# An edge-gated graph kernel: additions a tile ahead, edge sums two steps behind, z kept in the rows of h

## The chip, the cores and the metric

The kernel runs on one core of a Trainium2 chip. The metric is the time of one execution on the device in microseconds (us): the median of seven runs for the kernel before. One further execution was taken by the profiler, and all lines of the profile come from it.

Engines are named as in the profile: PE is TensorE (matmul), PEld its weight loads, DVE is VectorE, ACT is ScalarE, POOL is GpSimd and SP is SyncE, which here only issues DMA transfers. L12 is line 12 of the kernel.

## The reference

x is 16 batches of 1024 nodes with 256 features; adj is a sparse 1024 x 1024 matrix (about nine entries a column). Cut to what matters:

```python
pre_u = einsum('bud,dk->buk', x, W1[:256])
pre_v = einsum('bvd,dk->bvk', x, W1[256:])
hidden = relu(pre_u[:, :, None, :] + pre_v[:, None, :, :] + b1)
S = sigmoid(einsum('buvk,ko->buvo', hidden, W2)[..., 0] + b2)
a = einsum('buv,bud->bvd', S * adj, x)          # gated edge sums
m = einsum('uv,bud->bvd', adj, x) * x            # plain edge sums, times x
out = beta1 * x + beta2 * (a @ Wa + ba) + beta3 * (m @ Wm + bm)
```

S is needed only where adj has an entry, so the kernel works on lists of edges.

## The kernel before, in words

**Tiling.** The 16 batches form 4 groups of 4 (g), the 1024 target nodes 8 blocks of 128 (vt). A block (g, vt) is worked on as 10 tiles of up to 128 edges each: two windows of 64 targets (w), five tiles a window (j). There are 32 blocks and 320 tiles; tile n is tile s = n % 10 of block k = n // 10. Of the 32 blocks, 0 to 15 belong to groups 0 and 1, 16 to 23 to group 2 and 24 to 31 to group 3.

**A tile.** `fetch` (L496, an indirect DMA issued by POOL) gathers for each edge one row of 8 KB out of a table in DRAM: 1024 numbers of pre_u (four batches) and the 1024 numbers of x. The rows land in one of NF = 6 buffers `fetched`. `expand` (L569, two matmuls) spreads pre_v + b1 of the targets (`X`) over the edges into PSUM (`pc`, two buffers). `gate` adds both into `t` (L601), and four operations `t = max(t, 0) * W2` with an accumulated sum give a score for each edge and batch (L606). ScalarE takes the sigmoid (L609) and scales the columns of `left`, which already hold the edge's adj value (`left_adj`, L579), by it (L612). `aggregate` (L623) multiplies `left` with the x half of the fetched rows and sums over edges in PSUM (`acc`).

**A block.** `half_end` (L631) copies a finished `acc` to SBUF (`ev`), `turn_over` transposes it on TensorE (L641), copies the result into `LT` (L644) and later multiplies the plain sums by x (`times_h`, L654). `block_end` multiplies `LT` with Wa and Wm (L672) into a PSUM tile `pz`, ScalarE copies that to `z` (L675), VectorE adds beta1 * h (L676) from the rows `h_blk` loaded by SP (L775), and SP stores z (L678).

**Work laid beside it.** `halves` makes X for the next block (products L427 and L431, copies L461, L462, L465, L468, subtraction L463). `rows` makes pre_u for a table that a later block fetches from (product L427, copy L443, store L446); its place is written out by hand in `plan`, as (load of x transposed, first half, second half), for blocks up to tile 233. `lists` makes the edge lists of a target block, in pieces that `fill` puts between the operations of `gate`.

**The order.** Every engine's instructions run in the order in which the loop over n writes them; there is no scheduler. `after(step, f)` puts f into a queue that `do(step)` runs. PSUM for products, transposes and pz is a pool of two banks (`misc`, made by `small`); a new tile takes a bank whose last tile has been read, as far as the order written so far says.

In step n the kernel before writes the edge sums of tile n - 1 (and the fetch for tile n + 5, which takes the buffer just read), the gate of tile n, then `do(n)`, the expansion for tile n + 2, and after these the transposes, products and their copies:

```python
        if 1 <= n <= total:
            aggregate(n - 1)
            fetch_val(2)
            if n - 1 + NF < total:
                fetch(n - 1 + NF)
            ...
        if n < total:
            gate(n)
```

Of the kernel before, what the change touches and what calls it, by code (L numbers as in the profile page):

```python
# [17 lines left out]
def kernel(  # L18
# [207 lines left out]

    NF = 6
    EARLY = 4  # L230
    fetched = []
    for i in range(NF):
# [146 lines left out]
    def fetch_val(n):  # L379

        for i, j in wanted[:n]:
            nc.gpsimd.indirect_dma_start(  # L382
                out=val[:, i, j:j + 1], out_offset=None, in_=adj_flat,
                in_offset=bass.IndirectOffsetOnAxis(ap=vidx[:, i, j:j + 1], axis=0),
                bounds_check=N * N - 1, oob_is_err=False)
        del wanted[:n]
# [12 lines left out]
    def after(step, f):  # L399
        due.setdefault(step, []).append(f)  # L400
# [191 lines left out]
    def fill(n, gap=True):  # L592
        for r in running:
            if r[1] == gap and r[2] <= n:
                piece_of(r, n)
                break

    def gate(n):
        k, g, vt, w, j = where(n)
        t = one.tile([P, GB, D], FP, name="t")  # L600
        nc.vector.tensor_tensor(t, fetched[n % NF][:, :GD].rearrange("p (b d) -> p b d", b=GB),  # L601
                                pcs.pop(n).rearrange("p (b d) -> p b d", b=GB), ALU.add)
        sc = wk.tile([P, GB], FP, name="sc")
        for b in range(GB):
            fill(n)
            nc.vector.scalar_tensor_tensor(t[:, b, :], t[:, b, :], 0.0, w2_b,  # L606
                                           ALU.max, ALU.mult, accum_out=sc[:, b:b + 1])
        gt = wk.tile([P, GB], FP, name="gt")
        nc.scalar.activation(gt, sc, AF.Sigmoid, bias=b2_b)  # L609
        for b in range(GB):  # L610
            m = len(QUARTERS[j])
            nc.scalar.activation(lefts[n][:, :m, b, 1, :], lefts[n][:, :m, b, 0, :], AF.Copy, scale=gt[:, b:b + 1])  # L612
# [15 lines left out]
    def half_end(n, q):  # L628

        evs[q] = one.tile([P, 2, D], FP, name=f"ev{q}")  # L630
        nc.scalar.copy(evs[q], accs.pop(q))  # L631

    def turn_over(k, w, q, step):
        if w == 0 and q == 0:
            LTs[k] = one.tile([P, DC, GB, 2, P], FP, name="LT")
        LT = LTs[k]
        pt = small("pt")
        ev = evs.pop(q)
        for i in range(4):
            r, c = divmod(i, DC)  # L640
            nc.tensor.transpose(pt[:, i * P:(i + 1) * P], ev[:, r, c * P:(c + 1) * P], ident)  # L641
        v = slice(w * W + q * U, w * W + (q + 1) * U)
        r = (w * W + q * U) // V
        nc.scalar.copy(LT.rearrange("p c b k (r v) -> p r (c b k) v", v=V)[:, r:r + 2],  # L644
                       pt.rearrange("p (r i v) -> p r i v", r=2, v=V))
        apart = k == BS - 1 and w == NW - 1
        if not apart:
            if not q:
                return
            v = slice(w * W, (w + 1) * W)  # L650

        def times_h():
            m = LT[:, :, :, 0, v]
            nc.vector.tensor_tensor(m, m, hTs[order[k]].rearrange("p b c n -> p c b n")[:, :, :, v], ALU.mult)  # L654
            if w == NW - 1 and q == 1:
                del hTs[order[k]]
        after(step + (1 if k == BS - 1 else 2), times_h)

    def block_end(k):

        g, vt = order[k]
        hb = hbs[k]
        z = big.tile([P, GB, D], FP, name="z", bufs=1)
        for h in range(2):
            for i, wt in ((1, w_a), (0, w_m)):
                step = yield
                if i:
                    pz = small("pz")
                    add_row(pz, bias_p)
                for bb in range(2):  # L670
                    for c in range(DC):
                        nc.tensor.matmul(pz[:, bb * D:(bb + 1) * D], LTs[k][:, c, 2 * h + bb, i, :], wt[:, c, :],  # L672
                                         start=False, stop=(i == 0 and c == DC - 1), skip_group_check=True)
            sl = slice(2 * h, 2 * h + 2)
            nc.scalar.copy(z[:, sl], pz.rearrange("p (b d) -> p b d", b=2))  # L675
            after(step + 2, lambda sl=sl: nc.vector.scalar_tensor_tensor(z[:, sl], hb[:, sl], be1, z[:, sl],  # L676
                                                                         ALU.mult, ALU.add))
        after(step + 3, lambda: nc.sync.dma_start(  # L678
            out[g * GB:(g + 1) * GB, vt * P:(vt + 1) * P, :].rearrange("b p d -> p b d"), z))
        del hbs[k], LTs[k]  # L680


# [43 lines left out]
    def plan(blocks, ns):  # L726

        for k, (load, *pieces) in zip(blocks, ns):
# [4 lines left out]
                     (43, 50, 52)))  # L733
    plan([(2, vt) for vt in range(NT)], ((60 + 10 * i, 68 + 10 * i, 71 + 10 * i) for i in range(NT)))
    plan([(3, vt) for vt in range(NT)], ((141, 149, 151), (149, 158, 161), *((153 + 10 * i, 161 + 10 * i, 168 + 10 * i)
                                                                             for i in range(2, NT - 1)), (223, 231, 233)))
    plan(again, ((103,), (113,), (125,), (133,)))
    begun = set(turn[:NT])
    end = parts = piece = last = None
# [2 lines left out]
        expand(n)  # L742
    left_adj(0)
    total = BS * T
    for n in range(total + 2):
        k, s = divmod(n, T)
        if 1 <= n <= total:
            aggregate(n - 1)
            fetch_val(2)
            if n - 1 + NF < total:  # L750
                fetch(n - 1 + NF)
            if n % TW in (0, MID + 1):
                half_end(n - 1, 0 if n % TW else 1)
        if n < total:
            gate(n)
            if n + 1 < total:
                left_adj(n + 1)
        if n % TW == 1 and n // TW + 1 < total // TW:
            load_mark(n // TW + 1)
        do(n)  # L760
        if n + 2 < total:
            expand(n + 2)
        if n == 1:
            w_a = load_weights(Wa, "w_a", nc.sync)
            w_m = load_weights(Wm, "w_m", nc.sync)
            bias = load_rows(bm, D, "bias", nc.sync)
            ba_b = load_rows(ba, D, "ba_b", nc.sync)
            be1 = load_rows(beta1, 1, "be1", nc.sync)
            be2 = load_rows(beta2, 1, "be2", nc.sync)
            be3 = load_rows(beta3, 1, "be3", nc.sync)  # L770
            after(10, scale_late)
        if s == 0 and 0 < k < BS:
            hbs[k - 1] = big.tile([P, GB, D], FP, name="h_blk", bufs=1)
            g, vt = order[k - 1]
            nc.sync.dma_start(hbs[k - 1], x_rows[vt * P:(vt + 1) * P, g * GB:(g + 1) * GB, :])  # L775
        if n == total - 6:
            hbs[BS - 1] = hts.tile([P, GB, DC, P], FP, name="hT").rearrange("p b c n -> p b (c n)")
            for v, m, f in tails:
                for h, o in tail_rows(x, v, m, f):
                    nc.sync.dma_start(h, o)  # L780
        for i in advance.get(n, ()):
            next(made[i], None)
        if n in start_list:
            running.append([made[start_list[n]], True, n])
            piece_of(running[-1], n)
        fill(n, False)
        if (s == 1 and 0 < k < BS) or n == total:
            turn_over(k - 1, 1, 1, n)
        if s in (3, 4, 5, 6) and 0 < k < BS:
            if s == 3:  # L790
                end = block_end(k - 1)
                next(end)
            go(end, n)
        if s == 7 and k < BS:
            turn_over(k, 0, 0, n)
            turn_over(k, 0, 1, n)
        if s == 9 and k < BS:
            turn_over(k, 1, 0, n)
        if n == total - 2:
            end = tail(tails[:2], n)  # L800
            next(end)
        elif n == total - 1:
            go(end, n)
        elif n >= total:
            end = tail([tails[2 + n - total]], n)
            next(end)
            go(end, n)
            go(end, n)
        if k + 1 < BS and s in (0, 2, 3, 5, 6):
            if s == 0:  # L810
                parts = halves(k + 1)
                next(parts)
            go(parts, n)
        if n in loads:
            if loads[n] in begun and loads[n][0] == 1:
                aside_.remove(loads[n])
            load_hT(loads[n])
            if loads[n] not in begun:
                copy_h(loads[n])
                begun.add(loads[n])  # L820
        if n in at:
            if at[n] != last:
                last = at[n]
                piece = rows(last)
                next(piece)
            go(piece, n)
        if n == 120:
            nc.gpsimd.partition_all_reduce(longest, rest, P, bass_isa.ReduceOp.max)
            after(n + 12, count_rest)
# [114 lines left out]
```

## Time and profile before

| What | Value |
|---|---|
| median of 7 runs | 1168.84 us (1165.89 to 1171.88) |
| profiled execution: time, span | 1167.33 us, 1165.4 us |
| busy share PE, DVE, ACT, POOL | 94%, 91%, 77%, 38% |
| mean granted TensorE clock | 0.976 |
| DMA: bytes, mean rate | 391.40 MB, 336 GB/s |

The span is the time from the first to the last instruction. The profile's page gives the busy time of each engine and the costliest groups of instructions, each with its count, its mean duration and the idle time before it with what ended that. The windows view gives busy times for stretches of the span. The timeline gives each instruction's start and duration, equal ones that follow each other merged ("x8"); in brackets stands idle time before it and what ended it. Matmuls are pipelined and their ends modelled, so TensorE's work is best read from starts. The waits view has lines "engine tile line <- what ended the wait: us in total, times, longest us".

### The profile page before, as it was taken

What the parts mean: (1) busy time and instruction counts of PE and PEld (TensorE: products, weight loads), DVE (VectorE), ACT (ScalarE), POOL (GpSimd) and SP (SyncE); (2) the same over time, 40 slices, a digit from 0 to 9 for tenths busy, and PEclk for the clock granted to TensorE, in tenths of its full rate; (3) what the DMA queues carried; (4) which work ended last, traced back from release to release, by engine and by line L of the source; (5) the groups of instructions that cost most, each with busy time, mean ns of one, the idle gap of its engine ahead of it and who ended that gap; (6) DMA issues with size and microseconds to landing.
All of it is one profiled execution on the core that took longest, in us unless ns stands there. A gap on an engine that the chain in (4) does not pass through costs nothing. (4 is left out here: it accounts for less than half of the span.)

```text
span 1165.4 us, 23918 instructions
## 1 busy us (share of the span) xinstructions
PE 1092.9 (94%) x7633; PEld 723.5 (62%) x7633; DVE 1056.3 (91%) x3487; ACT 894.2 (77%) x2624; POOL 439.6 (38%) x428
## 2 busy tenths in 40 slices
PE   7767899998999999999999999999999999999986
PEld 6644666665666666666666666666666666666553
DVE  7688889878999989989999999999999999999994
ACT  2346587777877877878888888888888888888873
POOL 1557645263335323443333333333333333333330
PEclk9968899999999999999999999999999999999999
DMA  9996899999999999999999999999999999999992
GB/s 283 304 311 221 276 379 335 346 307 344 355 313 331 381 380 337 361 345 384 386 370 367 363 366 356 359 372 380 361 373 339 357 325 334 333 340 328 326 338 69
DMA packets 147047, 391.40 MB, mean 336 GB/s; under 512 B 16752, under 2 KB 105328, under 8 KB 110704
## 3 DMA queue, kind: packets, MB, share of 16 engines
q0 software_dynamic: 50016, 300.50, 69.3%
q1 hardware_dynamic: 81616, 74.99, 20.1%
q10 hardware_dynamic: 15280, 14.29, 3.8%
q8 instruction: 63, 1.03, 0.4%
q14 instruction: 72, 0.59, 0.1%
HBM read 393.78 MB, written 50.33 MB: 381 GB/s over the span
## 5 line engine op out<-in xcount | busy, mean ns | idle before, releaser
L496 POOL DMA_INDIRECT fetched<-table,uidx x320 | 340.3, 1064 | 628.3 <-PE acc L623 463.5
L606 DVE SCALAR_TENSOR_TENSOR t<-t,w_b 128x256 f32<-128x256 f32 x1280 | 478.7, 422 | 19.3 <-ACT left L612 0.5
L601 DVE TENSOR_TENSOR t<-fetched,pc 128x1024 f32<-128x1024 f32 x320 | 389.5, 1217 | 42.9 <-PE pc L569 10.7
L623 PE MATMUL acc<-fetched,left 128*32 128x256 f32 x4096 | 335.6, 391 | 32.5 <-ACT left L612 26.8
L612 ACT ACTIVATE left<-left,gt 128x32 f32<-128x32 f32 (+1 forms) x1280 | 299.3, 304 | 10.4
L569 PE MATMUL pc<-X,mark 128*128 128x512 f32 x640 | 238.4, 455 | 6.2 <-ACT mark L562 5.0
L623 PEld LDWEIGHTS acc<-fetched,left 128*32 128x32 f32 x4096 | 129.8, 109 | 180.0 <-issue 55.4
L569 PEld LDWEIGHTS pc<-X,mark 128*128 128x128 f32 x640 | 97.3, 191 | 140.1 <-issue 88.1
L609 ACT ACTIVATE gt<-sc,b_b 128x4 f32<-128x4 f32 x320 | 96.2, 301 | 40.5 <-DVE t L606 35.9
L672 PE MATMUL misc<-w_m,LT 128*128 128x256 f32 x496 | 117.2, 379 | 0.0
L672 PE MATMUL misc<-w_a,LT 128*128 128x256 f32 x496 | 117.1, 379 | 0.0
L579 ACT ACTIVATE left<-onehot,val 128x128 f32<-128x128 bf16 (+1 forms) x320 | 116.5, 364 | 0.0
L427 PE MATMUL misc<-w_v,hT 128*128 128x256 f32 x448 | 107.4, 383 | 0.0
L427 PE MATMUL misc<-w_u,hT 128*128 128x256 f32 x416 | 101.4, 391 | 5.6 <-issue 3.6
L606 DVE DVE_READ_ACCUMULATOR t<-t,w_b 128x1 f32 x1280 | 104.3, 81 | 0.0
L672 PEld LDWEIGHTS misc<-w_a,LT 128*128 128x128 f32 x496 | 93.9, 189 | 15.1
L672 PEld LDWEIGHTS misc<-w_m,LT 128*128 128x128 f32 x496 | 93.8, 189 | 14.9
L382 POOL DMA_INDIRECT val<-in_adjT_dram,vidx x80 | 86.5, 1081 | 34.9 <-issue 22.0
L427 PEld LDWEIGHTS misc<-w_v,hT 128*128 128x128 f32 x448 | 86.0, 192 | 13.9
L427 PEld LDWEIGHTS misc<-w_u,hT 128*128 128x128 f32 x416 | 80.1, 196 | 17.2 <-issue 3.7
L631 ACT COPY ev<-acc 128x512 f32<-128x512 f32 x128 | 75.5, 590 | 14.1 <-PE acc L623 3.7
L641 PE MATMUL misc<-ident,ev 128*128 128x128 f32 x512 | 74.0, 276 | 5.6 <-ACT L L342 2.8
(164 smaller groups left out, 911.7 us busy)
## 6 DMA issues: line engine op xcount, KB each, us to landing
h_blk<-in_x_dram SPq DMA_DIRECT2D x31, 512.0 KB
out_dram<-z SPq DMA_DIRECT2D x31, 512.0 KB
hT<-in_xT_dram SPq DMA_DIRECT2D x28, 512.0 KB
table<-in_x_dram ACTq DMA_DIRECT2D x24, 512.0 KB
table<-tab SPq DMA_DIRECT2D x24, 512.0 KB
fetched<-table,uidx POOLq DMA_INDIRECT x320
table<-in_x_dram SPq DMA_DIRECT2D x8, 512.0 KB
table<-fetched SPq DMA_DIRECT2D x8, 512.0 KB
```

Source lines behind the costliest of these rows:

```text
L382: nc.gpsimd.indirect_dma_start(out=val[:, i, j:j + 1], out_offset=None, in_=adj_flat, in_offset=bass.IndirectOffsetOnAxis(ap=vidx[:, i, j: ...
L427: nc.tensor.matmul(p[:, bb * D:(bb + 1) * D], hT[:, 2 * h + bb, i, :], wt[:, i, :], start=(i == 0 and not begun), stop=(i == DC - 1), skip ...
L496: nc.gpsimd.indirect_dma_start(out=fetched[n % NF], out_offset=None, in_=table[g], in_offset=bass.IndirectOffsetOnAxis(ap=uidx[:, vt * NW ...
L569: nc.tensor.matmul(pcs[n][:, c], marks[n // TW][:, j * P:(j + 1) * P], cuts[k][:, w, c], start=True, stop=True)
L579: nc.scalar.activation(lefts[n][:, :m, :, 0, :], onehot[:, i, o:o + m, :].unsqueeze(2).to_broadcast([P, m, GB, V]), AF.Copy, scale=val[:, ...
L601: nc.vector.tensor_tensor(t, fetched[n % NF][:, :GD].rearrange("p (b d) -> p b d", b=GB), pcs.pop(n).rearrange("p (b d) -> p b d", b=GB), ...
L606: nc.vector.scalar_tensor_tensor(t[:, b, :], t[:, b, :], 0.0, w2_b, ALU.max, ALU.mult, accum_out=sc[:, b:b + 1])
L609: nc.scalar.activation(gt, sc, AF.Sigmoid, bias=b2_b)
L612: nc.scalar.activation(lefts[n][:, :m, b, 1, :], lefts[n][:, :m, b, 0, :], AF.Copy, scale=gt[:, b:b + 1])
L623: nc.tensor.matmul(accs[h][b * 2 * V:(b + 1) * 2 * V, r, :], left[:, i, b].rearrange("p k v -> p (k v)"), f[:, GD + b * D:GD + (b + 1) * D ...
L631: nc.scalar.copy(evs[q], accs.pop(q))
L672: nc.tensor.matmul(pz[:, bb * D:(bb + 1) * D], LTs[k][:, c, 2 * h + bb, i, :], wt[:, c, :], start=False, stop=(i == 0 and c == DC - 1), sk ...
```

## The change

- **Two steps behind.** In step n the edge sums of tile n - 2 are written, no longer those of n - 1. At the end the loop returns to one step behind.
- **Addition ahead and in place.** The addition of tile n + 1 is an operation of its own (`add`) written just before the gate of tile n, and its output goes into the fetched rows; `t` is that place.
- **Seven buffers** for fetched rows.
- **Order in a step.** Transposes, products and their copies are written ahead of the gate, and `do(n)` after it. Three transposes move with this: those of (w = 1, first half) from s = 9 to s = 0 of the next block, those of (w = 1, second half) from s = 1 to s = 2; `times_h` of the latter runs after one step rather than two.
- **z in the rows of h.** ScalarE's copy of pz is gone. VectorE reads pz itself, a step earlier, and writes into `h_blk`, which is then stored; the tile z is gone.
- The last entry of the plan is (222, 230, 232).

The diff, cut:

```diff
-    NF = 6
+    NF = 7
...
+    def add(n):
+        t = fetched[n % NF][:, :GD]
+        nc.vector.tensor_tensor(t, t, pcs.pop(n), ALU.add)
+
     def gate(n):
         k, g, vt, w, j = where(n)
-        t = one.tile([P, GB, D], FP, name="t")
-        nc.vector.tensor_tensor(t, fetched[n % NF][:, :GD].rearrange("p (b d) -> p b d", b=GB),
-                                pcs.pop(n).rearrange("p (b d) -> p b d", b=GB), ALU.add)
+        t = fetched[n % NF][:, :GD].rearrange("p (b d) -> p b d", b=GB)
...
-        after(step + (1 if k == BS - 1 else 2), times_h)
+        after(step + (1 if k == BS - 1 or w else 2), times_h)
...
-        z = big.tile([P, GB, D], FP, name="z", bufs=1)
...
-            nc.scalar.copy(z[:, sl], pz.rearrange("p (b d) -> p b d", b=2))
-            after(step + 2, lambda sl=sl: nc.vector.scalar_tensor_tensor(z[:, sl], hb[:, sl], be1, z[:, sl],
-                                                                         ALU.mult, ALU.add))
+            after(step + 1, lambda sl=sl, pz=pz: nc.vector.scalar_tensor_tensor(
+                hb[:, sl], hb[:, sl], be1, pz.rearrange("p (b d) -> p b d", b=2), ALU.mult, ALU.add))
         after(step + 3, lambda: nc.sync.dma_start(
-            out[g * GB:(g + 1) * GB, vt * P:(vt + 1) * P, :].rearrange("b p d -> p b d"), z))
+            out[g * GB:(g + 1) * GB, vt * P:(vt + 1) * P, :].rearrange("b p d -> p b d"), hb))
...
+    def gather_in(n):
+        aggregate(n)
+        fetch_val(2)
+        if n + NF < total:
+            fetch(n + NF)
+        if (n + 1) % TW in (0, MID + 1):
+            half_end(n, 0 if (n + 1) % TW else 1)
+
     for n in range(total + 2):
         k, s = divmod(n, T)
+        if 2 <= n < total - 2:
+            gather_in(n - 2)
+        if total - 3 <= n <= total:
+            gather_in(n - 1)
         if n % TW == 1 and n // TW + 1 < total // TW:
             load_mark(n // TW + 1)
-        do(n)
         if n + 2 < total:
             expand(n + 2)
+        if n >= total - 2:
+            do(n)
-        if (s == 1 and 0 < k < BS) or n == total:
+        if (s == 2 and 0 < k < BS) or n == total:
             turn_over(k - 1, 1, 1, n)
         if s in (3, 4, 5, 6) and 0 < k < BS:
             (block_end of block k - 1, one of its four parts in each step)
         if s == 7 and k < BS:
             turn_over(k, 0, 0, n)
             turn_over(k, 0, 1, n)
-        if s == 9 and k < BS:
-            turn_over(k, 1, 0, n)
+        if (s == 0 and 0 < k < BS) or n == total - 1:
+            turn_over(k - (s == 0), 1, 0, n)
...
         (halves in s = 0, 2, 3, 5, 6, loads and rows of the plan)
+        if n + 1 < total:
+            add(n + 1)
+        if n < total:
+            gate(n)
+            if n + 1 < total:
+                left_adj(n + 1)
+        do(n)
         (weights at n = 1, load of h_blk at s = 0, pieces of the lists)
```

More of the change, by code (lines that the diff above doesn't have):

```diff
@@ L735 @@
     plan([(3, vt) for vt in range(NT)], ((141, 149, 151), (149, 158, 161), *((153 + 10 * i, 161 + 10 * i, 168 + 10 * i)
-                                                                             for i in range(2, NT - 1)), (223, 231, 233)))
+                                                                             for i in range(2, NT - 1)), (222, 230, 232)))
     plan(again, ((103,), (113,), (125,), (133,)))
@@ L744 @@
     total = BS * T
+    add(0)
+    def gather_in(n):
[5 more added lines that the diff above has]
+            half_end(n, 0 if (n + 1) % TW else 1)
     for n in range(total + 2):
         k, s = divmod(n, T)
[L747 to L757, printed above, removed]
+        if 2 <= n < total - 2:
+            gather_in(n - 2)
+        if total - 3 <= n <= total:
+            gather_in(n - 1)
         if n % TW == 1 and n // TW + 1 < total // TW:
             load_mark(n // TW + 1)
-        do(n)
         if n + 2 < total:
             expand(n + 2)
[L763 to L786, printed above, removed]
-        if (s == 1 and 0 < k < BS) or n == total:
+        if n >= total - 2:
+            do(n)
+        if (s == 2 and 0 < k < BS) or n == total:
             turn_over(k - 1, 1, 1, n)
@@ L826 @@
             go(piece, n)
+        if n + 1 < total:
[5 more added lines that the diff above has]
+        do(n)
+        if n == 1:
+            w_a = load_weights(Wa, "w_a", nc.sync)
+            w_m = load_weights(Wm, "w_m", nc.sync)
+            bias = load_rows(bm, D, "bias", nc.sync)
+            ba_b = load_rows(ba, D, "ba_b", nc.sync)
+            be1 = load_rows(beta1, 1, "be1", nc.sync)
+            be2 = load_rows(beta2, 1, "be2", nc.sync)
+            be3 = load_rows(beta3, 1, "be3", nc.sync)
+            after(10, scale_late)
+        if s == 0 and 0 < k < BS:
+            hbs[k - 1] = big.tile([P, GB, D], FP, name="h_blk", bufs=1)
+            g, vt = order[k - 1]
+            nc.sync.dma_start(hbs[k - 1], x_rows[vt * P:(vt + 1) * P, g * GB:(g + 1) * GB, :])
+        if n == total - 6:
+            hbs[BS - 1] = hts.tile([P, GB, DC, P], FP, name="hT").rearrange("p b c n -> p b (c n)")
+            for v, m, f in tails:
+                for h, o in tail_rows(x, v, m, f):
+                    nc.sync.dma_start(h, o)
+        for i in advance.get(n, ()):
+            next(made[i], None)
+        if n in start_list:
+            running.append([made[start_list[n]], True, n])
+            piece_of(running[-1], n)
+        fill(n, False)
         if n == 120:
```

## The prediction

> **What bounds the kernel now.** I read the page's busy shares first, then the windows view cut where the kind of block changes, then the timeline inside one block. A block is ten tiles, and s (0 to 9) is a tile's place in it.
>
> ```profile
> PE 1092.9 (94%) x7633; PEld 723.5 (62%) x7633; DVE 1056.3 (91%) x3487; ACT 894.2 (77%) x2624; POOL 439.6 (38%) x428
> ```
> ```profile
> 71.10:268.80 197.70, 180.10 (x1168) 120.16 (x1167) 171.42 (x589) 138.31 (x403) 106.39 (x102) 0.93 0.90 309
> 268.80:545.90 277.10, 267.69 (x1890) 176.78 (x1889) 258.37 (x861) 223.34 (x660) 108.09 (x104) 0.99 0.96 353
> 545.90:897.60 351.70, 349.71 (x2531) 230.01 (x2529) 333.19 (x1049) 297.81 (x886) 118.86 (x110) 1.00 0.99 367
> 897.60:1147.80 250.20, 239.84 (x1741) 151.43 (x1741) 240.40 (x760) 206.25 (x629) 79.98 (x77) 1.00 0.90 325
> ```
> Columns: window, its length, busy PE, PEld, DVE, ACT, POOL, granted clock, DMA share, GB/s. The cuts are the first L601 rows of blocks 0, 5, 13 and 24 and the end of the last L606. So there are five blocks of 39.5 us, eight of 34.6, eleven of 32.0 and eight of 31.3. TensorE, VectorE and the DMA engines are all near full, so no share alone names the bound. The timeline does, first VectorE in block 27:
>
> ```profile
> 1002.95 0.69 DVE L654 TENSOR_TENSOR LT<-LT,hT 128x512 f32<-128x512 f32 x1
> 1003.55 1.22 DVE L601 TENSOR_TENSOR t<-fetched,pc 128x1024 f32<-128x1024 f32 x1
> 1004.80 0.43 DVE L606 SCALAR_TENSOR_TENSOR t<-t,w_b 128x256 f32<-128x256 f32 x1
> ...
> 1006.19 1.22 DVE L463 TENSOR_TENSOR low<-low,X 128x1024 f32<-128x1024 f32 x1
> 1007.33 1.21 DVE L601 TENSOR_TENSOR t<-fetched,pc 128x1024 f32<-128x1024 f32 x1
> ...
> 1009.62 0.42 DVE L606 SCALAR_TENSOR_TENSOR t<-t,w_b 128x256 f32<-128x256 f32 x1
> ...
> 1010.14 1.22 DVE L601 TENSOR_TENSOR t<-fetched,pc 128x1024 f32<-128x1024 f32 x1
> 1011.46 0.42 DVE L606 SCALAR_TENSOR_TENSOR t<-t,w_b 128x256 f32<-128x256 f32 x1
> ```
> Read the starts, not the durations. L463 (the same 1024 columns as L601) lets its successor start after 1.14 us. L601, whose successor reads the t it writes, holds it for 1.25 to 1.32 (mean 1.285 over the middle of the trace). A product L606 lets an independent successor start after 0.35, but the next L601, which overwrites t, after 0.52. These waits count as nothing in the busy shares, yet in the last eight blocks VectorE has no other gap: it is their bound. TensorE in the same stage:
>
> ```profile
> 996.24 0.73 PE L569 MATMUL pc<-X,mark 128*128 128x512 f32 x2
> 996.81 0.60 PE L641 MATMUL misc<-ident,ev 128*128 128x128 f32 x4
> 998.00 1.69 PE L623 MATMUL acc<-fetched,left 128*32 128x256 f32 x16 [0.59 <-ACT left L612]
> 999.61 0.73 PE L569 MATMUL pc<-X,mark 128*128 128x512 f32 x2
> ```
> It waits for ScalarE's gates there. By start-to-start times where nothing waits, an L569 pair takes 0.57, the edge sums of a tile 0.57 (8 rows) or 1.00 (16), eight rows of a 256-column product 1.82, a bias row 0.23, four transposes 0.53 and eight 0.97. A block is 4 x 0.57 + 6 x 1.00 + 10 x 0.57 + 6 x 1.82 + 4 x 0.23 + 2 x 0.53 + 0.97 = 27.9. Blocks up to 23 also make a table's rows, 2 x 1.82 more: 31.5, and the quickest of them take 31.4. So blocks 13 to 23 stand on TensorE and VectorE alike, and 24 to 31 on VectorE with 3.4 us of TensorE to spare. Blocks 5, 6, 9 and 10 (38.2, 34.8, 38.0 and 34.8) carry list work on VectorE.
>
> **The change part by part.**
>
> *Addition a tile ahead.* No L606 follows the addition it reads, and no addition overwrites what was just read. Per quiet block VectorE loses 10 x (1.285 - 1.138) = 1.47 and, at the five tiles with no operation between, 5 x (0.52 - 0.35) = 0.87: 2.3 us, 31.3 to 29.0. In blocks with lists I count 1.2 to 1.5, since list operations already stand in these places. In-place output costs nothing: L606 is in place now.
> [...]
>
> *Two steps behind.* Written out engine by engine, the new order repeats the old cycle with the gates' index shifted by one. TensorE still alternates edge sums and expansion, and the fetch for tile n+5 is still released in step n. The seventh place pays for the earlier addition, so the lead of a fetch (11 to 13 us from issue to use, its packets done after about 7) stays; POOL's queue keeps its order, its 463.5 us of waiting for L623 being the buffers' turn. Evacuation of acc (L631, 128 x 0.59) now stands behind a gate, not ahead of it. List operations of VectorE fall a tile later against TensorE, ScalarE and DMA, which covers most of
>
> ```profile
> DVE s_of L346 <- ACT L L342: 7.9, 3, 3.0
> ...
> DVE key L249 <- DMA key<-in_adjT_dram: 6.5, 2, 3.3
> ```
> *Copies ahead of the gates.* ScalarE's cycle is again old, gate then copies. But transposes and products now share steps 0 and 2, and step 9 has none. After the rows of s = 8, the tab copy (0.59), sigmoid (0.30) and four gatings (0.93), 1.82 in all, must fit beside TensorE's step 9, 1.57 long: with handovers about 0.35 of waiting per block, zero to 0.6.
>
> *z in the rows of h.* ScalarE loses 62 copies
>
> ```profile
> L675 ACT COPY z<-misc 128x512 f32<-128x512 f32 x62 | 36.4, 586 | 54.3 <-PE misc L672 38.5 <-PE acc L623 11.4 <-PE pc L569 2.7
> ```
> and the 54 us for which its queue stood before them. VectorE reads pz from PSUM instead. L601 with a PSUM operand (1217 ns) and L463 without (1221) price that at 0 per instruction.
> [...]
> Two costs follow. First, pz stays in its bank until VectorE's step s + 1. In the changed program both groups of transposes of s = 7 get the same bank, as pz of the second half still holds the other; now they run as eight in 0.97. The second group must wait for ScalarE to empty the first: 0.27 until the last transpose is written, 0.03 to L644, its 0.575, and 0.07 back to TensorE, less the 0.11 pitch: 0.85, say 0.9 us on TensorE in each block. Behind it queue the next edge sums and expansion. Where TensorE bounds, this is added in full; where it has slack, it is partly hidden. Second, h_blk's load now waits on SP until the store from the same rows has landed. The store leaves about a tile earlier, and eight tiles (25 us) remain until L676. By the packets' times in the trace the two moves of 512 KB took 6 us together from 703.8 and 19 us in a crowded stretch (735 to 754). In blocks 6 to 13 the 512-byte packets of hT (10 to 25 us) now stand ahead of it on SP's queue. I take 2 us in all, between 0 and 8.
>
> *Moved with these.* w_m's products (s = 4) now wait for L654 of step 3, which ends some 2 us after the addition that the preceding expansion waits for; that expansion starts 1.7 to 4.8 us after it. No cost. The 222/230/232 plan loads, converts and stores as many bytes.
>
> **The sum**, on the profiled execution: span 1165.4, run 1167.3, which is 1.5 below the median of seven.
> - Blocks 24 to 31: VectorE 29.0, TensorE 27.9 + 0.9 = 28.8. Two floors so close and uneven steps (4.2 us of TensorE at s = 0, 1.6 at s = 9) do not meet: following the ten steps by hand I lose about 1, mostly at s = 6 to 8. 30.0, so -1.3 x 8 = -10 (-18 to +3).
> - Blocks 13 to 23: TensorE 31.4 + 0.9 + 0.35 = 32.7 against 32.0: +8 (-6 to +14).
> - Blocks 7, 8, 11, 12: 32.8 on average, a few waits go and these come: 0 (-4 to +4).
> - Blocks 5, 6, 9, 10: the key waits (6.5) and 1.2 to 1.5 each go, TensorE then holds at 33.5 to 35.2: -8 (-12 to 0).
> - Blocks 0 to 4: TensorE at half clock for part of blocks 0 and 1 (0.93 mean), three tables' halves a block: -5 (-10 to +5).
> - h_blk +2; the end, where the change returns to one step behind, +0.5; the first 71 us, 0.
> Together -13: 1154 for the execution, 1155.5 on the median.
>
> **Rivals.**
> 1. *All pauses vanish in the slack.* ScalarE frees 36 us of copies and 54 of standing before them, so gates come early and the blocks reach the larger floor: -17, -4, -4, -11, -8: about 1125. For it: blocks 18, 20 and 25 to 27 already sit within 0.2 us of their floors. Against: TensorE's 0.9 cannot be hidden where TensorE bounds.
> 2. *Slower: the shared bank at s = 7 and the uneven steps.* If each block pays 0.9 + 0.35 on TensorE and, in 13 to 31, half a microsecond more of ScalarE queueing, then blocks 13 to 23 give +14, 24 to 31 0, the list blocks -4, the early ones +1: +11, 1180. It decides from about 0.7 us a block beyond my sum. For it: DMA and PE shares of 0.99 in that stage. Against: the ScalarE waits that go.
> 3. *The ordering stall does not go away*, because what delays L606 is not the data but a switch of shapes. Then VectorE stays at 31.3 and only list waits go: about -8 + 8 + 3 = +3, 1172. Against: L463 to L601 and L654 to L601 show full overlap across kinds.
>
> **Numbers.** Forecast 0.49, rival 1 0.19, rival 2 0.20, rival 3 0.12. The measurement tells 0.3% (3.5 us) from none. Forecast's own range is 1144 to 1166; with the rivals' ends 1126 to 1178. Faster: 0.46 of the forecast and 0.19 = 0.65; the same: 0.03 and 0.06 of rival 3 = 0.09; slower: 0.20 and 0.06 = 0.26.
>
> **What would show it.** After: L600 to L608 starts 1.14 apart; DVE busy time nearly unchanged but for less idle; no L675-like copy; the two transposes of s = 7 apart by 0.9 us with a wait on ScalarE's LT copy; last eight blocks near 30.0, blocks 13 to 23 near 32.7; key waits gone. I am wrong if L676 waits on h_blk, if additions wait on fetches, or if the late blocks stay at 31.3.

## The result and the profile after

The changed kernel takes 1174.27 us (median of 27 runs, 1168.09 to 1186.51) against 1168.59 for the kernel before (69 runs): ratio 1.005, 95% interval 1.0035 to 1.0064. It is half a per cent slower, where 1.1% faster was forecast. Ratios, here and below, leave out the runs of a kernel that lie over 1.5% above its fastest one, while medians and ranges are of all its runs. The profiled execution has a span of 1168.7 us, 3.3 more than before.

The first line is the page's busy shares. The rows after it are the windows view, cut as in the prediction (first L600 of blocks 0, 5, 13 and 24, end of the last L608), with the end of the kernel as a fifth row; the columns are those of the prediction.

```profile
PE 1076.5 (92%) x7633; PEld 706.9 (60%) x7633; DVE 1025.3 (88%) x3487; ACT 855.8 (73%) x2562; POOL 439.6 (38%) x428
```
```profile
70.66:273.59 202.93, 178.67 (x1149) 117.58 (x1149) 164.97 (x580) 131.78 (x391) 105.16 (x101) 0.92 0.87 300
273.59:545.16 271.57, 260.07 (x1885) 171.25 (x1884) 250.76 (x863) 212.63 (x640) 109.33 (x104) 1.00 0.98 359
545.16:903.61 358.45, 348.57 (x2539) 227.17 (x2540) 323.46 (x1049) 286.71 (x868) 115.53 (x111) 1.00 0.99 361
903.61:1147.58 243.97, 232.61 (x1731) 145.28 (x1732) 233.17 (x768) 197.08 (x617) 81.91 (x77) 0.99 0.93 334
1147.58:1168.72 21.14, 10.21 (x128) 5.29 (x124) 2.56 (x6) 3.03 (x9) 0.00 (x0) 0.82 0.12 30
```

Against before: blocks 0 to 4 +5.2, blocks 5 to 12 -5.5, blocks 13 to 23 +6.8, blocks 24 to 31 -6.2, the end +3.5 (17.6 before); the first 71 us -0.4. TensorE, VectorE and ScalarE are busy for less time and the kernel is longer: read alone, the first line would say "faster". VectorE in block 27, from its timeline, shows that the planned part works:

```profile
1007.39 0.71 DVE L656 TENSOR_TENSOR LT<-LT,hT 128x512 f32<-128x512 f32 x1
1008.02 1.21 DVE L600 TENSOR_TENSOR fetched<-fetched,pc 128x1024 f32<-128x1024 f32 x1
1009.15 0.41 DVE L608 SCALAR_TENSOR_TENSOR fetched<-fetched,w_b 128x256 f32<-128x256 f32 x1
...
1010.53 1.21 DVE L463 TENSOR_TENSOR low<-low,X 128x1024 f32<-128x1024 f32 x1
1011.67 1.21 DVE L600 TENSOR_TENSOR fetched<-fetched,pc 128x1024 f32<-128x1024 f32 x1
```

A product L608 now starts 1.13 after the addition ahead of it (mostly 1.24 to 1.33 before), because it reads another tile's sum. Part of what took the gain is in TensorE's timeline. The first two rows are from before (block 17, s = 7), the other four from after (block 16, s = 6 and 7; a bracket is idle time before the row, and what ended it):

```profile
701.04 1.03 PE L641 MATMUL misc<-ident,ev 128*128 128x128 f32 x8
702.01 1.23 PE L623 MATMUL acc<-fetched,left 128*32 128x256 f32 x13
```
```profile
671.10 0.73 PE L569 MATMUL pc<-X,mark 128*128 128x512 f32 x2
671.66 0.60 PE L643 MATMUL misc<-ident,ev 128*128 128x128 f32 x4
672.94 0.66 PE L643 MATMUL misc<-ident,ev 128*128 128x128 f32 x4 [0.68 <-ACT LT L646]
673.52 0.85 PE L625 MATMUL acc<-fetched,left 128*32 128x256 f32 x12
```

The second group of transposes stands for ScalarE's copy of the first, since both use one bank: from the first transpose to the next edge sums it is 1.86 (671.66 to 673.52), where it was 0.97. And it is in the waits view of the whole kernel (in us total, times, longest); the first row is from before, the other two from after.

```profile
DVE t L601 <- PE pc L569: 10.7, 13, 2.0
```
```profile
DVE fetched L600 <- PE pc L569: 72.8, 87, 7.8
...
PE misc L643 <- ACT LT L646: 15.6, 23, 0.8
```

VectorE has become the engine that waits, for TensorE.

### The profile page after: what moved, and what is told of

It reads as the page before. It is cut to its first block, busy times and chain, and to the rows that moved or that the text cites. A ratio compares the mean times of both kernels' runs of the same rounds, so it can differ in the third digit from the quotient of the medians.

```text
span 1168.7 us, 23884 instructions
## 1 busy us (share of the span) xinstructions
PE 1076.5 (92%) x7633; PEld 706.9 (60%) x7633; DVE 1025.3 (88%) x3487; ACT 855.8 (73%) x2562; POOL 439.6 (38%) x428
## 4 chain that ended last, share of the span: by engine, by line
PE 73%; ACT 9%; DVE 9%; issue 4%; DMA 3%; another core or an unknown queue 1%; ACTq 0%; POOL 0%; DVEq 0%; POOLq 0%
PE acc L625 20%; PE misc L427 17%; PE misc L673 15%; PE pc L569 14%; PE misc L643 5%; DVE fetched L608 3%; PE misc L431 2%; DVE fetched L600 2%; DMA table<-tab 2%; ACT left L614 2%; ACT LT L646 1%; ACT gt L611 1%; DMA fetched<-in_adjT_dram 1%; ACT X L461 1%
## 5 line engine op out<-in xcount | busy, mean ns | idle before, releaser
L600 DVE TENSOR_TENSOR fetched<-fetched,pc 128x1024 f32<-128x1024 f32 x320 | 388.4, 1214 | 99.1 <-PE pc L569 72.8
L608 DVE SCALAR_TENSOR_TENSOR fetched<-fetched,w_b 128x256 f32<-128x256 f32 x1280 | 474.4, 416 | 0.0
L625 PE MATMUL acc<-fetched,left 128*32 128x256 f32 x4096 | 313.3, 390 | 19.2 <-ACT left L614 12.5
L625 PEld LDWEIGHTS acc<-fetched,left 128*32 128x32 f32 x4096 | 117.8, 109 | 161.7 <-issue 61.3
L633 ACT COPY ev<-acc 128x512 f32<-128x512 f32 x128 | 72.7, 568 | 40.5 <-PE acc L625 35.3
L643 PE MATMUL misc<-ident,ev 128*128 128x128 f32 x512 | 79.4, 278 | 24.3 <-ACT LT L646 15.6
L646 ACT COPY LT<-misc 128x512 f32<-128x512 f32 x128 | 73.4, 577 | 38.6 <-PE misc L643 28.6
L608 DVE DVE_READ_ACCUMULATOR fetched<-fetched,w_b 128x1 f32 x1280 | 100.2, 78 | 0.0
```

What stands on the lines that cost most here:

```text
L600: nc.vector.tensor_tensor(t, t, pcs.pop(n), ALU.add)
L625: nc.tensor.matmul(accs[h][b * 2 * V:(b + 1) * 2 * V, r, :], left[:, i, b].rearrange("p k v -> p (k v)"), f[:, GD + b * D:GD + (b + 1) * D ...
```

## The experiments

In the table, an experiment's ratio is against the kernel before on the same chip. The stages are in us, from the windows view of one execution each, cut as above. They scatter: e1 and e5 have the same order from block 6 on, and differ by 0.5 in blocks 24 to 31, by 6.5 in 5 to 12 and by 11 in 13 to 23. So a verdict on the whole time goes by the ratio, and one on a stage by its quick blocks or by several executions. "Quick" are here the blocks of 13 to 23 that make a table's rows, wait for no late transfer and so repeat one length, by the additions' starts.

| Kernel | ratio (95%) | 0-4 | 5-12 | 13-23 | 24-31 | end |
|---|---|---|---|---|---|---|
| before | 1 | 197.7 | 277.1 | 351.7 | 250.2 | 17.6 |
| after | 1.0050 (1.0035-1.0064) | 202.9 | 271.6 | 358.4 | 244.0 | 21.1 |
| e1 transposes apart | 0.9914 (0.9887-0.9940) | 202.6 | 269.5 | 352.6 | 237.4 | 18.6 |
| e2 rows apart | 0.9974 (0.9950-0.9999) | 195.9 | 273.5 | 360.8 | 244.4 | 18.5 |
| e3 one behind | 1.0083 (1.0051-1.0116) | 210.0 | 276.9 | 353.6 | 247.5 | 19.0 |
| e4 gates first | 1.0032 (1.0007-1.0058) | 203.2 | 283.9 | 353.3 | 239.9 | 19.0 |
| e5 = e1 + e2 | 0.9855 (0.9808-0.9902) | 191.1 | 276.0 | 363.5 | 237.9 | 18.8 |
| e6 = e5 + copies | 0.9977 (0.9949-1.0005) | 192.9 | 271.3 | 363.9 | 241.4 | 20.2 |
| e7 = e5, add beside | 0.9975 (0.9949-1.0001) | 193.5 | 273.1 | 356.5 | 248.0 | 17.5 |
| e8 = e5, copies early | 0.9910 (0.9879-0.9940) | 198.6 | 274.6 | 345.8 | 237.5 | 20.2 |
| e9 = e5, gates first | 0.9887 (0.9852-0.9923) | 189.6 | 273.1 | 354.8 | 239.6 | 18.6 |
| c1 before, rows moved | 1.0071 (1.0045-1.0098) | 215.1 | 276.2 | 352.2 | 250.2 | 17.6 |
| z alone on before | 1.0007 (0.9985-1.0029) | 201.1 | 275.2 | 350.6 | 250.8 | 17.8 |

**e1: the shared bank.**

```diff
         if s == 7 and k < BS:
             turn_over(k, 0, 0, n)
+        if s == (7 if k == BS - 1 else 9) and k < BS:
             turn_over(k, 0, 1, n)
```

> The changed kernel, but the second group of transposes of s = 7 (first window, second half) is written in s = 9, where TensorE has no other product; the last block keeps them in s = 7. Theory: in the changed kernel this group takes the same PSUM bank as the first and stands on ScalarE's copy for 0.9 us in every block, with the next edge sums behind it. Apart, that wait is gone and steps 7 and 9 are more even: blocks 13 to 23 fall from 32.54 to about 31.6 each, blocks 24 to 31 from 30.19 to 29.3 to 29.5, blocks 0 to 12 by about 0.5 each: 10 + 6 + 6 = 22 us less than the changed kernel, about 1152. Rival: the wait only shows what some other queue (VectorE's or ScalarE's) would cost anyway; then blocks 24 to 31 stay at 30.2, blocks 13 to 23 fall by 0.3 at most, and the time is 1168 to 1172.

The ratio falls from 1.0050 to 0.9914, by 16 us. The windows of blocks 13 to 23 and 24 to 31, and TensorE in block 16 again, now with four transposes at s = 7 (664.76) and four at s = 9 (668.77), neither waiting:

```profile
541.84:894.49 352.65, 345.77 (x2548) 227.59 (x2547) 322.11 (x1051) 285.30 (x867) 119.07 (x110) 1.00 0.99 367
894.49:1131.87 237.38, 231.36 (x1742) 146.00 (x1737) 232.49 (x770) 197.35 (x616) 83.50 (x76) 1.00 0.94 344
```
```profile
664.76 0.60 PE L643 MATMUL misc<-ident,ev 128*128 128x128 f32 x4
665.28 1.07 PE L625 MATMUL acc<-fetched,left 128*32 128x256 f32 x16
...
668.77 0.60 PE L643 MATMUL misc<-ident,ev 128*128 128x128 f32 x4
669.29 1.07 PE L625 MATMUL acc<-fetched,left 128*32 128x256 f32 x16
```

By the additions' starts the quick blocks of 13 to 23 take 31.40 each, 0.1 below the prediction's count of TensorE's work (31.5), and blocks 24 to 30 take 29.30. In the changed kernel they take 32.54 and 30.19. So bank and place together cost 1.14 in the one stage and 0.89 in the other. The edit changes both: the two groups now take 0.52 each instead of 1.86 together, which is 0.82, and four transposes move into a step that had no product. This run alone does not divide the gain between the two; e4 helps below. The rival, that some other queue would take the gain, falls for the quick blocks. The sum of blocks 13 to 23 gained only 6, not 10, because two of them (15 and 19) are 2 and 7 us longer than the quick ones; e6 and e8 are on that.

**e2: crowded steps in the first blocks, and c1, its control.** The same edit is made in the changed kernel (e2) and in the kernel before (c1):

```diff
-    ((0, 5, 8), (6, 12, 15), (12, 18, 22), (17, 25, 28), (24, 32, 35), (31, 38, 42), (38, 45, 48), (43, 50, 52))
+    ((0, 4, 8), (6, 11, 14), (12, 18, 21), (17, 24, 28), (24, 31, 34), (31, 38, 41), (38, 44, 48), (43, 50, 51))
```

> The changed kernel, but in the first 52 tiles the products that make a table's rows are moved from s = 2, 5 and 0 to s = 1, 4, 8 and 9, where neither transposes nor halves are written (plan entries 5, 12, 15, 22, 25, 32, 35, 42, 45, 52 become 4, 11, 14, 21, 24, 31, 34, 41, 44, 51). Theory: blocks 0 to 4 grew because transposes, a half of X and rows now stand in one step, so that the next edge sums and expansion come late and VectorE's additions wait for the expansion (27 us in the profile of the changed kernel); apart, blocks 0 to 4 fall from 203 to 195 to 198 us together, the rest stays: about 1167. Rival: the early blocks are slow for another reason (half clock, a load of h_blk, code loading), and stay within 2 us of 203: about 1174.

> The kernel before with nothing but the moved rows of the first 52 tiles (same entries as in the repair). Theory: the crowding is of the change's making, since only there transposes share steps 0 and 2 with halves and rows; in the kernel before the old places have no transposes, and the new places at s = 1 and 9 have. Then blocks 0 to 4 stay at 198 or grow by up to 3: 1168 to 1172. Rival: the old plan was bad already and the repair would have helped without the change; then blocks 0 to 4 fall to about 191 to 194 and the time to 1162 to 1165.

e2: 1.0050 to 0.9974, 9 us; blocks 0 to 4 at 195.9, the time at 1167.9, both as the theory has them. c1: 1.0071, so the kernel before loses 8 us by the very edit from which the changed one gains 9, more than expected. (c1's profiled execution is the slowest of its runs, so its 215 overstates.) A good place for rows is not one of the plan alone: it depends on where the transposes stand, and the change moved those and left the plan. One crowded step, s = 2 of block 1 in the changed kernel, first TensorE, then VectorE:

```profile
127.69 0.80 PE L431 MATMUL misc<-b_p,unit 128*128 128x512 f32 x1 [4.05 <-issue]
128.29 3.62 PE L427 MATMUL misc<-w_v,hT 128*128 128x256 f32 x8
133.07 3.78 PE L427 MATMUL misc<-w_u,hT__973 128*128 128x256 f32 x8 [1.16 <-ACT low L462]
136.78 1.10 PE L625 MATMUL acc<-fetched,left 128*32 128x256 f32 x16
137.81 0.73 PE L569 MATMUL pc<-X,mark 128*128 128x512 f32 x2
```
```profile
130.08 0.69 DVE L656 TENSOR_TENSOR LT<-LT,hT 128x512 f32<-128x512 f32 x1
138.58 1.22 DVE L600 TENSOR_TENSOR fetched<-fetched,pc 128x1024 f32<-128x1024 f32 x1 [7.82 <-PE pc L569]
```

A half of X and a table's rows stand between one expansion and the next, at half clock (granted 0.50 from 128.29 to 136.78; 3.62 and 3.78 for eight rows that take 1.89 where it is 1.00), the second of them waiting for the bank, and VectorE stands 7.8 us for its next addition. The 4.05 ahead of L431 is not of this kind: VectorE and ScalarE stand until 127 us too, and the trace names no engine that ended it. The waits view of the first five blocks gives the additions' wait for the expansion, before, after, in e2 and in c1, in this order:

```profile
DVE t L601 <- PE pc L569: 5.3, 5, 2.0
```
```profile
DVE fetched L600 <- PE pc L569: 27.1, 12, 7.8
```
```profile
DVE fetched L600 <- PE pc L569: 14.9, 11, 2.8
```
```profile
DVE t L601 <- PE pc L569: 20.7, 10, 5.5
```

That row alone follows the stage badly: it is 16.2 in e1, where blocks 0 to 4 take 202.6, and 19.7 in e5, where they take 191.1. All of VectorE's waits for TensorE in this stage, added up, do better: 29 to 30 us with the old places (after, e1, e4), 21 to 25 with the new ones (e2, e5, e6, e8, e9). That is 4 to 9 of the 10 us; the rest of the path is not shown. The granted clock does not explain the stage: at 0.92 it takes 202.9 in the changed kernel and 193.5 in e7.

**e3: is the second step of distance needed?** In the kernel before: `add` written ahead of `gate` as in the change, NF = 7, z in the rows of h, plan entry 222/230/232; the rest as before.

> The kernel before with three parts of the change alone: addition a tile ahead and in place, seven places, z in the rows of h (and the last plan entry 222/230/232). Edge sums stay one step behind, gates stay ahead of ScalarE's copies, transposes stay in s = 1, 7, 9. Theory: the gain of the change is the addition ahead (2.3 us of VectorE a block), and its losses belong to the two steps behind and the new order (shared bank at s = 7, copies ahead of gates, crowded steps 0 and 2). Then blocks 24 to 31 come to 29.0 to 29.5, blocks 13 to 23 to 31.5 to 31.8, the first five to about 193, the end as before (17.6): 1135 to 1145. Rival: without the second step of distance TensorE stands on the gates for what VectorE saves, so that blocks 24 to 31 stay at 31 and 13 to 23 at 32: 1163 to 1168.

1.0083: the theory is wrong, and the time is above even the rival's. Blocks 24 to 30 take 30.81, the quick ones of 13 to 23 31.91, blocks 0 to 4 are the second longest of all. ScalarE's gates wait for VectorE for 100.7 us (35.9 before):

```profile
ACT gt L611 <- DVE fetched L608: 100.7, 133, 3.8
```

With the addition of tile n + 1 ahead of gate n, the edge sums of tile n come an addition (1.1 us) later, and the next expansion stands behind them in TensorE's order. The second step of distance takes them out of that chain. This chain is argued from the order and not shown: the row above reads 111.7 in e9, which is fast, and 85.0 where z alone is changed, at no loss. Measured is that the addition ahead loses in this order, and pays in e5 and e7 below, which have the second step, but another order in a step and other places of rows as well. No run has the second step as its only difference.

**e4: ScalarE's order.** The changed kernel, with the lines from `add(n + 1)` to `left_adj(n + 1)` moved up, ahead of the transposes, products and copies.

> The changed kernel, but addition, gate and the left rows of a step are written ahead of its transposes, products and copies, as before the change, so that ScalarE does its gates ahead of the copies of the same step; do(n) stays at the step's end, so that the shared bank at s = 7 stays too. Theory: copies ahead of gates make the end (21.1 us after the last product of VectorE, 17.6 before) and part of the first five blocks longer, since gates stand behind copies that wait for TensorE: the end falls by 2 to 3, blocks 0 to 4 from 203 to about 198. The first copy at s = 7 now stands behind a sigmoid and four gatings, so TensorE's wait there grows by up to 0.9 a block: blocks 13 to 23 come to 32.8 to 33.4. Sum 1169 to 1174. Rival: the order on ScalarE is of no account in the early blocks, TensorE's own order is; then blocks 0 to 4 stay at 203 and the time is 1174 to 1182.

1.0032, not to be told from the changed kernel's 1.0050; blocks 0 to 4 stay at 203.2. The order on ScalarE is not what slows the first blocks. The premise was wrong in one point: in this kernel the two groups of transposes do not wait for each other (its waits view has no row of L643 for L646), and run as eight, 1.20 to the next edge sums (1.86 in the changed kernel, 0.97 before):

```profile
651.63 1.27 PE L643 MATMUL misc<-ident,ev 128*128 128x128 f32 x8
652.83 1.07 PE L625 MATMUL acc<-fetched,left 128*32 128x256 f32 x16
```

Blocks 13 to 23 and 24 to 31 gain 5 and 4 for it, and blocks 5 to 12 lose 12, which in e9 they don't. The transposes take 0.66 less, and the blocks of equal length take 31.96 and 29.54, which is 0.58 and 0.65 less. So without the bank's wait, but with all eight at s = 7, about half of e1's 1.14 is gained in blocks 13 to 23 and most of its 0.89 in 24 to 30. If the order on ScalarE counts for as little here as between e5 and e9, the rest is the move to s = 9, together with the 0.23 by which the eight still take longer than before. So e4 tells two things apart badly; it stands as a second case of gain without the shared bank.

**z in the rows of h, alone on the kernel before.**

> The kernel before with z in the rows of h alone: ScalarE's 62 copies of pz are gone, VectorE reads pz itself a step earlier, the store leaves from h_blk; six places, order and additions as before. Theory: in the kernel before VectorE bounds blocks 24 to 31 and ScalarE's copies lie beside it, so taking 36 us from ScalarE alone moves these blocks by 0 to 0.3 each, and the loads of h_blk behind the store cost 0 to 4: 1164 to 1170. Rival: ScalarE's standing before these copies (54 us) delays gates and with them TensorE; then blocks 13 to 31 each gain 0.3 to 0.6, about 1158 to 1163.

1.0007 (1169.0 us; -1.8 to +3.4 us by the interval): nothing that shows, and blocks 24 to 31 stay at 31.4 each. Together, ScalarE's freed copies and the load of h_blk behind the store come to about nothing; the run does not tell whether each does. In the changed kernel VectorE waits 2.7 us for that load.

**e5: both repairs.**

> Both repairs together: the second group of transposes of s = 7 in s = 9, and the rows of the first 52 tiles in steps without transposes and halves. They act in different stages, so the theory adds them: against the changed kernel the first gave 1.35% and the second 0.75%, so 1.005 becomes about 0.984 of the kernel before, about 1150 us; blocks 0 to 4 at 196 us together, blocks 24 to 31 at 29.3 each. Rival: with less waiting the DMA engines (share 0.99 in blocks 13 to 23) take back what one repair gives; then it stays at 0.990.

0.9855 (median 1157.2 us), as the sum of the two repairs: it beats both kernels, by 1.5% and 1.9%. Its interval is wide, since its six runs scatter (1144.9 to 1177.3; before 1163.3 to 1175.3), and in its profiled execution blocks 13 to 23 are long. The median of all six is only 1.0% below the kernel before.

**e7: what the addition ahead is worth.** e5 with `add(n)` just ahead of `gate(n)`.

> Both repairs, but the addition of tile n is written just ahead of the gate of tile n again (in place, seven places, two steps behind as before). Theory: a product that reads what the addition ahead of it wrote starts 1.285 instead of 1.138 after it, so VectorE's floor of blocks 24 to 31 goes from 29.0 to 30.5 and these blocks from 29.3 to 30.5 or 30.8: 9 to 12 us more there; blocks 13 to 23 stay, bounded elsewhere. Rival: the stall is not of the data; then nothing changes in blocks 24 to 31.

0.9975: 1.2% (0.7 to 1.7) of 1169, 14 us, are lost again; by the medians of all runs it is 6.5. In the profiles 10 us of it lie in blocks 24 to 31, where all but the last repeat one length: 30.68 against 29.30, within the 30.5 to 30.8 expected. A product mostly starts 1.24 to 1.33 after the addition it reads, as in the kernel before. The rows are blocks 24 to 31 in e5 and in e7, and an addition with its product in e7:

```profile
901.12:1139.05 237.93, 231.65 (x1742) 145.94 (x1737) 232.51 (x770) 197.22 (x616) 83.40 (x76) 1.00 0.94 343
```
```profile
892.37:1140.37 248.00, 231.64 (x1742) 145.06 (x1735) 237.38 (x762) 196.02 (x609) 81.59 (x75) 0.99 0.90 326
```
```profile
1000.22 1.21 DVE L600 TENSOR_TENSOR fetched<-fetched,pc 128x1024 f32<-128x1024 f32 x1
1001.54 0.43 DVE L608 SCALAR_TENSOR_TENSOR fetched<-fetched,w_b 128x256 f32<-128x256 f32 x1
```

**e6 and e8: are the DMA engines the bound of blocks 13 to 23?** The first adds to e5 a transfer that nothing reads, the second moves transfers out of these blocks:

```diff
+        if s == 5 and 13 <= k <= 23:                       # e6
+            nc.scalar.dma_start(spare, x_rows[:P, :GB, :])
...
+        if n in range(4, 52, 6):                           # e8
+            copy_h((3, (n - 4) // 6))
+            begun.add((3, (n - 4) // 6))
```

> Both repairs, and in blocks 13 to 23 one more transfer of 512 KB a block from x to a spare place in DRAM that nothing reads (issued on ScalarE's queue at s = 5, like the copies into the tables). Theory: in these blocks the DMA engines are the bound now. All variants but the unrepaired one take 352 to 354 us there at 366 to 367 GB/s; by that rate 512 KB are 1.4 us, so eleven of them add 13 to 18 us to blocks 13 to 23 (352 to 365 or more). Rival: TensorE bounds these blocks (31.4 in the quick ones) and the DMA share only shows queues kept full; then the transfers cost ScalarE's issue, 0.56 each, at most: 0 to 5 us.

> Both repairs, and the eight copies of 512 KB from x into the tables of group 3 are issued at tiles 4, 10, ... 46 instead of tiles 141 to 222, in the blocks whose DMA share is 0.88. Theory: the DMA engines bound blocks 13 to 23; they have 4 MB less there, 11 us at 367 GB/s, so these blocks fall from about 352 to 343 to 346, where TensorE holds them (31.4 a block, less where no rows are made); blocks 0 to 4 grow by 0 to 5. Sum 3 to 9 us below both repairs alone. Rival: TensorE bounds blocks 13 to 23, nothing changes there, and the early blocks lose up to 5.

e6 is 1.2% (0.7 to 1.8) slower than e5: 14 us, at the lower end of what the DMA bound asks and well above the rival's 5. Its profiled execution doesn't show it against e5's, which was long there itself, but does against e1's and e9's (363.9 against 352.6 and 354.8). In e8 blocks 13 to 23 take 345.8, the shortest of all, and all but the last take at most 31.7 (TensorE's count is 31.5):

```profile
545.72:891.55 345.83, 344.21 (x2548) 226.28 (x2547) 322.78 (x1051) 284.99 (x867) 117.94 (x110) 1.00 0.99 362
```

But the first blocks pay 7 for it, and the ratio, 0.991, is no better than e5's. Where e5 loses time in blocks 13 to 23, the waits view of that stage names transfers (in e8 the first wait is 2.2 and the second 0.7):

```profile
ACT tab L443 <- DMA table<-tab: 10.5, 3, 5.1
...
DVE h_blk L676 <- DMA h_blk<-in_x_dram: 5.3, 2, 3.2
```

So, with the bank apart, late transfers hold up some of these blocks in the profiled executions. That the DMA engines set a floor for the whole stage is supported by e6 and not settled by e8.

**e9: gates first, on both repairs.**

> Both repairs, and additions, gates and left rows written ahead of a step's products and copies. Theory: with the two groups of transposes apart no copy is waited for at once, so in blocks 13 to 31 the order on ScalarE is of no account (31.4 and 29.3 in the quick blocks); in the list blocks 5 to 12 copies ahead of gates help TensorE, as in the unrepaired pair (272 with copies ahead, 284 with gates ahead), so the time is 8 to 14 us longer than with both repairs: 0.992 to 0.997 of the kernel before. Rival: the 284 was of that one execution; then the time is that of both repairs, 0.985, or better by the 0.5 us a block by which gates ahead made the unrepaired late blocks quicker.

0.9887 (0.9852 to 0.9923): between the two expectations, and not to be told from e5. Blocks 5 to 12 take 273.1, not 284. ScalarE's order is worth nothing that these runs can show.

## Why the prediction was wrong

Forecast was -13 on the profiled execution, measured +3.3 on its span, 16 off. Of these 10 lie in blocks 0 to 4, 4 in blocks 24 to 31 and 3 in the end; the rest nearly cancels. On the medians it is 1155.5 against 1174.3. The prediction's small sums are up to 0.02 us off (0.27 + 0.03 + 0.575 + 0.07 - 0.11 is 0.835, 5 x 0.17 is 0.85), which changes nothing.

- **Blocks 0 to 4, forecast -5, measured +5.2: the step that failed.** The measured value lies just outside the -10 to +5 that the prediction allowed there. It named the half clock and "three tables' halves a block", and costed the moved transposes only where it found them, in quiet blocks; beside the early rows it put them at nothing. It did not lay the early plan over the new order, although the plan's places (12, 22, 32, 42, 52 are all s = 2) stand in the text of the kernel. With the rows moved away, blocks 0 to 4 take 190 to 196 in e2, e5, e6, e7 and e9, 192.6 on average: the -5 that was forecast. (In e8, which moves copies there, they take 198.6.) The places of the rows are worth 10 in the profiles and 9 by the ratios of after and e2, and turned a small gain (0.9974) into a loss.
- **Blocks 24 to 31, forecast -10, measured -6.2.** VectorE's floor was right: 29.30 in e1, without the bank's wait, against 29.0. With the wait a block takes 30.19, near the 30.0 that the prediction reached by adding a loss of 1 to the floors (8 x 0.19 is 1.5 us). The other 2.4 are block 31, 32.64 to the last L608, where the end begins (30.62 before).
- **Blocks 13 to 23, forecast +8, measured +6.8.** Right in size: 32.54 in the quick blocks against 32.7, and the wait as priced (1.86 - 0.97 is 0.89, where 0.9 was forecast). e1 shows that bank and place cause it: 1.14 of the 1.25 forecast for the two (0.9 + 0.35). That the stage's total fits so well has some luck: blocks 17 and 18 take 30.2 and 30.8, and block 23 takes 36.8.
- **Blocks 5, 6, 9 and 10: forecast -8, measured -8.7; blocks 7, 8, 11 and 12: 0, measured +3.2** (-4 to +4 given). h_blk's load: +2 forecast; L676 waited 2.7 us for it in all.
- **The end, forecast +0.5, measured +3.5.** The chain of waits shows two LT copies, one after the other, and then the last gates behind them:

```profile
1141.05 0.59 ACT LT L646
...
1141.69 0.67 PE misc L643 x4
...
1142.38 0.59 ACT LT L646
1142.97 0.20 ACT gt L611
...
1143.20 0.33 ACT left L614
...
1143.57 2.55 PE acc L625 x16
```

  "Return to one step behind" meets "copies ahead of gates" at s = 7 of the last block. The last row is sixteen edge sums in 2.55, which take 1.07 elsewhere: the granted clock is 0.54 from 1143.57 to 1146.97. In e6 and e8 it is 0.50 and 0.53 in the last 3.4 us ahead of the end too, and the end takes 20.2. In e1, e2, e5 and e9 it is 1.00 there, and much the same end takes 18.5 to 18.8. So about 1 of the 3.5 is the order's, and the rest goes with the clock.
- **A sign that failed.** VectorE's busy time was to stay nearly unchanged and fell from 1056.3 to 1025.3. The durations of its records, added up, fall by only 14 us (1282.6 to 1268.7); the rest is overlap, which busy time counts once: an addition takes 1.21, and the product behind it now starts after 1.13.
- **Three prices that held.** The addition ahead, priced at 1.47 a block for its products' starts, gives 1.38 in blocks 24 to 31 (30.68 in e7, 29.30 with it) and 14 us in all by the ratios: a product starts 1.13 after the addition ahead of it, against 1.24 to 1.33 behind one that it reads. In place the addition takes 1214 ns, where it took 1217. VectorE's read of pz out of PSUM was priced at 0: L676 takes 740 ns with one source in PSUM and took 747 with both in SBUF.
- **The rivals.** Rival 3 falls with e7. Rival 2 had the right sign and, at 1180, too high a price: it asked half a microsecond a block of ScalarE queueing in blocks 13 to 31, which e9 does not show against e5 (31.39 in quick blocks of both, 29.35 against 29.30 in the last ones); what decided lay in blocks 0 to 4, where it allowed +1. Rival 1 needed the bank wait to hide in slack, and it is the part that e1 takes away.

## What to carry to other kernels

When an order written by hand is shifted, lay every other hand-written plan over the new order, stage by stage, and count what each engine does between two instructions that another engine waits for; here a plan for 52 tiles, untouched by the change, cost it 9 us. A buffer that is read a step later takes away a place from whoever comes next: look up which place the next users get, since two that shared nothing may then share one, as here two groups of transposes (1.86 us to the next edge sums, 0.97 before). VectorE's gain, 14 us by the ratios of e7 and e5, did not show in the changed kernel (1.0050), where its additions wait 72.8 us for TensorE: measure a gain with the known obstacles removed, as e5 and e7 do, before judging the idea.

## What was not expected of the hardware

- Taking 36 us of copies off ScalarE, with VectorE reading PSUM in their place, changed nothing that shows (1.0007), although its queue had stood 54 us before them.
- With both repairs the kernel scatters more: six runs of e5 lie between 1144.9 and 1177.3, 29 of before between 1163.3 and 1175.3. One profile a kernel can't say where the difference lies; in those of e1 and e5 a few blocks of 13 to 23 (33 to 39 us instead of 31.4) wait for a store from tab or a load of h_blk. What makes these transfers late in one run and not in another stays open.
